# Feed-forward sums ahead of the block transposes, and routing ahead of the preceding group's, in a decoder layer in fp32

## The chip, the cores and the metric

The kernel runs on one core of a Trainium2 chip. The metric is the device time of one execution in microseconds (us). Before the change three runs gave 887.11, 887.35 and 888.24, a median of 887.35. Everything is fp32. The engines are called PE (matrix multiply; PEld is its weight load), DVE (vector), ACT (activations), POOL (GpSimd) and SP, which here only issues DMAs.

## What is computed

A decoder layer over 4096 tokens of width 256: 16 sequences of 256. Three sub-layers follow one another, each added to its input and normalised. The reference, cut to what matters:

```python
x = layernorm(x + attn(x))            # tokens against fixed keys and values, relu squared
x = layernorm(x + xattn(x, ctx))      # 16 heads of 16, softmax over 256 context rows
x = layernorm(x + ffn(x))

# xattn: attn = gamma * q @ k.T * scale + delta * (ap * max(D, 0) + an * min(D, 0))
#        D = clip(frac[k] - frac[q], -0.2, 0.2); out = softmax(attn) @ v @ Wo.T + bo

def ffn(x):                           # width 1024, 8 experts that differ by a rank 4 term
    logits = x @ gate_W.T + gate_b
    top1 = argmax(softmax(logits))
    base = x @ wi_W.T + wi_b
    for i in range(8):
        inter = relu(base + (x @ lora_A[i].T) @ lora_B[i].T)
        out += (top1 == i) * (inter @ wo_W.T + wo_b)
```

## The kernel before, in words

The program writes its order out by hand: within an engine the instructions run in the order in which the source issues them, and across engines they wait by semaphores for what they read and for buffers to come free.

The first sub-layer takes about the first 260 us. After it comes the main loop, which this change concerns. An iteration n handles one group: four of the sixteen heads of one sequence, 64 groups in all (n = 0 to 63, and two more iterations to drain). Several stages of different groups are interleaved. Group n is `now`, n + 1 is `nxt`, n - 1 is `last`, n - 2 is `older`:

- `negative` (POOL, L642, some on ACT) writes the negative part of the bias into `neg`, `positive` (ACT, L654) the positive part into four PSUM banks, one a head. `neg` has three buffers.
- `logits` (PE, L664) adds q.k to those banks. `maxima` (DVE, L682) adds `neg` and takes the row's extreme, bank by bank. `subtract` (POOL, L733) takes the maximum off heads 2 and 3.
- For heads 2 and 3, PE transposes the rows (`turned`, L743) and ACT takes the exponential into `pT` (`exps`, L750). For heads 0 and 1 of the groups 14 to 61 (`direct`) ACT takes it first (`exp_rows`, L696), then `blocks` (L707) transposes in blocks of 32 on DVE into `z` (one buffer, or the idle `kT` for every other group) and SP writes it to DRAM (`away_z`, L712). In the next iteration `fetch` (L724), four DMAs, brings it back in its final order into the same `pT`. SP's queue is in order: a fetch waits there for the landing of its write.
- `attend` (PE, L764), two iterations on as a rule, multiplies with the values into a PSUM bank `V`, heads 0 and 1 first, and `keep` (DVE, L777) copies it out. SP collects sums and values (L574 to L600), POOL divides (L607), PE projects (L614).

From n = 15 on the feed-forward of a block of 512 tokens (`ff`) is woven in, eight iterations, parts 0 to 7, per block; such a period is called a round here, rounds 0 to 5, with part = (n - 15) mod 8. Parts 0 and 1 transpose the block (L857, copied by ACT, L860) and multiply by gate and lora_A (`gates`, L872; copied by ACT, L882). Part 2 routes: `route` transposes the gates' result on PE (L887) and finds the first largest of eight on DVE in seven steps, lg (L893), top (L898), hot (L901, L902), first (L904), hot (L905) and `um` (four instructions, L909), the lora part masked by it. `biased` (POOL, L865) adds a bias to x. `inner` (L945) is the first large product, in two halves, `turn_um` (PE, L919, ACT's copy L925) transposes um, `lora` (L958) adds its product, and L967 (ACT) and L971 (DVE) apply the relu. Parts 4 to 7 `finish` 128 tokens each: eight matmuls (L978, sixteen PE instructions) and on DVE an add of the result to x (L991) and its mean and variance (bn_stats L191, bn_aggr L192). In parts 5 and 7 the result lies in the bank V that attend uses, and attend is put off by an iteration. In part 7 `prep` computes mean and scale of the next block on DVE (L208 to L246, the last is `nm`) and ACT scales its rows by them (L251).

`tile_b` hands out three PSUM banks in turn, so a transpose or product waits until the use three before it has been read. The blocks transpose of groups in parts 0 and 1 is put off (`later`) to the next iteration, after the maxima there. So in part 2 DVE runs the maxima, the preceding group's transpose into z, the routing, then the present group's transpose into kT. In parts 4 to 7 it runs, near the end of the iteration, the transpose and then the add and statistics of finish.

## Time and profile before

| | |
|---|---|
| median of three runs | 887.35 us |
| profiled execution | 887.49 us, of it the span of the profile 885.7 |
| granted PE clock, mean | 0.999 of full speed |
| PE waits in the whole span, longest in sum | attend L764 for the add L991: 6.0 us in 6 |
| maxima L682 on DVE | 512, 420 ns each |
| blocks transpose L707 on DVE | 24 into z, 1244 ns each; 24 into kT, 1238 ns each |
| add of finish L991 | 32, 381 to 422 ns; bn_stats L191 417 ns, bn_aggr L192 182 ns |
| routing: lg, top, hot, hot, first, hot, um | 162, 186, 503, 594, 186, 398 ns and four of 284 ns, 8 times |
| subtract L733 on POOL | 65, 1909 ns each |

In a timeline each row is start, duration, engine, line, operation, what is written and from what, with the idle time before it and who ended it in brackets. Times are counted from the start of the span. "issue" in such brackets means that the profile names nobody. SPq is SP's queue of DMA issues; when a DMA lands is told by the last of the sixteen updates of its semaphore in the trace. The ends of matmuls are modelled, so the start of what follows is the safer mark.

### The profile page before, as it was taken

The page shows a single profiled execution, that of the slowest core. Times are in us where ns is not written, and L with a number is a line of the kernel's source. Part 1 is how long each engine was busy: PE and PEld are TensorE (multiplying, and loading weights), DVE is VectorE, ACT ScalarE, POOL GpSimd, SP SyncE. Part 2 cuts the span into 40 slices and gives each one's busy share as a digit, 9 for nine tenths or more (in the row PEclk, how much of TensorE's full clock was granted, in tenths as well). Part 3 has the DMA queues.
Part 4 walks back from the last instruction along what each step waited for, and adds up shares of the span by engine and source line. Part 5 has one row for each costly group of instructions (what it writes and reads, how often), then busy time and mean ns, then how long its engine had stood idle before and what let it go on. Part 6 is the DMA issues. An engine that isn't in the chain of part 4 may idle for free.

```text
span 885.7 us, 20853 instructions
## 1 busy us (share of the span) xinstructions
PE 862.4 (97%) x7708; PEld 513.1 (58%) x7708; DVE 693.3 (78%) x1975; ACT 577.0 (65%) x1012; POOL 466.6 (53%) x455
## 2 busy tenths in 40 slices
PE   8999999999999999999999999999999999999997
PEld 4334444444456776567547656754765675576655
DVE  6878899889779898769778877877887787777444
ACT  5766777777788788647747765774875577475111
POOL 1100223322479898656828765883976678374010
PEclk9999999999999999999999999999999999999999
DMA  5501101010001333454454536445453644642001
GB/s 139 159 1 43 54 24 44 31 49 1 8 8 48 99 98 110 139 162 149 158 155 150 158 129 184 151 155 168 138 164 133 193 151 135 181 149 102 28 7 41
DMA packets 70373, 92.94 MB, mean 105 GB/s; under 512 B 13824, under 2 KB 55296, under 8 KB 70272
## 3 DMA queue, kind: packets, MB, share of 16 engines
q1 hardware_dynamic: 69696, 91.35, 33.2%
q8 instruction: 61, 1.00, 0.5%
q14 instruction: 40, 0.33, 0.1%
q10 hardware_dynamic: 576, 0.26, 0.1%
HBM read 50.43 MB, written 39.58 MB: 102 GB/s over the span
## 4 chain that ended last, share of the span: by engine, by line
PE 44%; DVE 11%; issue 2%; POOL 1%; ACT 1%; DMA 0%; ACTq 0%; POOLq 0%; DVEq 0%
PE ps_l L945 9%; PE ps_b L978 6%; PE ps_l L664 5%; PE ps_v L764 5%; PE ps_b L743 4%; DVE neg L682 3%; PE ps_b L614 3%; PE ps_v L978 3%; PE ps_b L477 2%; PE ps_l L958 2%; DVE z L707 1%; PE ps_b L503 1%; PE ps_b L532 1%; POOL neg L733 1%; DVE dpos L547 1%
## 5 line engine op out<-in xcount | busy, mean ns | idle before, releaser
L682 DVE CUSTOM_DVE_ANT_0 neg<-ps_l,neg 128x256 f32<-128x256 f32 x512 | 181.5, 420 | 41.4 <-PE ps_l L664 38.3
L642 POOL TENSOR_SCALAR neg<-dneg,aneg,delta 128x512 f32<-128x512 f32 x252 | 198.9, 804 | 20.9 <-PE ps_b L743 10.0
L654 ACT ACTIVATE ps_l<-dpos,apos_d 128x512 f32<-128x512 f32 x256 | 172.2, 688 | 49.9 <-DVE mx L682 30.9
L354 DVE TENSOR_TENSOR pr<-pr 128x1024 f32<-128x1024 f32 x128 | 153.8, 1243 | 30.2 <-ACT pr L353 29.8
L733 POOL TENSOR_TENSOR neg<-neg,mx 128x1024 f32<-128x1024 f32 x65 | 124.0, 1909 | 85.4 <-DVE mx L682 84.3
L353 ACT ACTIVATE pr<-ps_a 128x1024 f32<-128x1024 f32 x128 | 125.0, 1026 | 53.0 <-PE ps_a L345 52.7
L345 PE MATMUL ps_a<-xnT,kT 64*64 64x512 f32 x1024 | 124.6, 593 | 1.0 <-ACT xnT L330 0.4
L364 PE MATMUL ps_v<-pr,vv 64*64 64x512 f32 x1024 | 122.7, 589 | 0.0
L945 PE MATMUL ps_l<-xt,wi 128*128 128x512 f32 x248 | 111.7, 596 | 0.2
L750 ACT ACTIVATE pT<-ps_b 128x512 f32<-128x512 f32 x160 | 87.4, 590 | 32.4 <-PE ps_b L743 30.9
L743 PE MATMUL ps_b<-ident,neg 128*128 128x128 f32 x640 | 87.1, 277 | 3.4 <-ACT pT L750 2.3
L743 PEld LDWEIGHTS ps_b<-ident,neg 128*128 128x128 f32 x640 | 71.5, 141 | 24.0 <-issue 6.2
L364 PEld LDWEIGHTS ps_v<-pr,vv 64*64 64x64 f32 x1024 | 45.0, 133 | 64.5 <-issue 54.6
L379 POOL TENSOR_TENSOR xt<-xt,half 128x512 f32<-128x512 f32 x15 | 19.1, 1274 | 119.8 <-ACT half L378 119.8
L419 POOL TENSOR_TENSOR hid<-hid,bo 128x256 f32<-128x256 f32 x32 | 43.6, 1366 | 71.8 <-ACT hid L251 71.8
L696 ACT ACTIVATE neg<-neg,mx 128x256 f32<-128x256 f32 x192 | 81.3, 498 | 0.0
L764 PE MATMUL ps_v<-pT,vaug 128*32 128x256 f32 x1024 | 74.3, 385 | 7.2 <-DVE x L991 6.0
L664 PE MATMUL ps_l<-kM,qT 32*64 32x256 f32 x2048 | 79.8, 388 | 0.0
L345 PEld LDWEIGHTS ps_a<-xnT,kT 64*64 64x64 f32 x1024 | 41.9, 133 | 65.3 <-issue 52.5
L945 PEld LDWEIGHTS ps_l<-xt,wi 128*128 128x128 f32 x248 | 45.6, 191 | 49.4 <-issue 44.6
L978 PE MATMUL ps_b<-wof,hT 128*128 128x256 f32 x304 | 68.4, 380 | 0.0
L524 POOL TENSOR_SCALAR kM<-keys,of_head 128x512 f32<-128x512 f32 x22 | 38.7, 1760 | 48.4 <-DVE keys L513 48.4
(137 smaller groups left out, 1183.3 us busy)
## 6 DMA issues: line engine op xcount, KB each, us to landing
pT<-away_z SPq DMA_DIRECT2D x192, 128.0 KB
away_z<-z SPq DMA_DIRECT2D x24, 512.0 KB
away_z<-kT SPq DMA_DIRECT2D x24, 512.0 KB
away_v<-raw SPq DMA_DIRECT2D x16, 512.0 KB
cT<-in_ctxT SPq DMA_DIRECT2D x16, 256.0 KB
v<-away_v SPq DMA_DIRECT2D x32, 128.0 KB
invs<-rows SPq DMA_DIRECT2D x16, 256.0 KB
x<-in_x SPq DMA_DIRECT2D x7, 512.0 KB
```

The lines of the kernel that those rows point to most:

```text
L345: nc.tensor.matmul(sc[64 * k : 64 * k + 64, h, :], lhsT=kT[64 * h : 64 * h + 64, q, hf * P + 64 * k : hf * P + 64 * k + 64], rhs=self.xnT[ ...
L353: nc.scalar.activation(pr, sc, AF.Relu)
L354: nc.vector.tensor_tensor(pr, pr, pr, ALU.mult)
L364: nc.tensor.matmul(self.acc[k][64 * h : 64 * h + 64, :], lhsT=vv[64 * k : 64 * k + 64, hf, 64 * q : 64 * q + 64], rhs=pr[64 * k : 64 * k + ...
L642: nc.gpsimd.tensor_scalar(self.neg[:, g], self.batch.dneg, aneg[:, h : h + 1], delta, ALU.mult, ALU.mult,)
L654: nc.scalar.activation(banks[g], self.batch.dpos.rearrange("p j k -> p (j k)"), AF.Copy, scale=apos_d[:, h : h + 1],)
L664: nc.tensor.matmul(banks[g][64 * h : 64 * h + 64, j * S : (j + 1) * S], lhsT=self.batch.qT[rows, self.o, j * P + 64 * h : j * P + 64 * h + ...
L682: nc.vector.tensor_tensor_reduce(out=self.t[:, g, j, :], in0=banks[g][:, j * S : (j + 1) * S], in1=self.neg[:, g, j, :], scale=-1.0 if min ...
L733: eng.tensor_tensor(rows, rows, top.to_broadcast([P, 4, S]), ALU.subtract)
L743: nc.tensor.transpose(ps[:, k * S + j * P : k * S + (j + 1) * P], self.t[:, g, j, k * P : (k + 1) * P], ident,)
L945: nc.tensor.matmul(self.banks[g], lhsT=wi[:, c, f * P : (f + 1) * P], rhs=self.xT[:, c, :], start=(c == 0), stop=False,)
L978: nc.tensor.matmul(ps[:, 0:C], lhsT=self.hT[f][:, j * P : (j + 1) * P], rhs=wof[:, f, :], start=(f == 0), stop=(f == FC - 1),)
```

## The change

Two pieces move; nothing is added or removed.

```diff
             if now:
                 now.maxima()
                 now.later = n >= FIRST and part in (0, 1)
+            if ff and part == 2:
+                ff.route()
             if last and last.direct and last.later:
                 last.blocks()
...
                     last.turned(g)
                     last.exps(g)
-                if part == 2:
-                    ff.route()
                 if now.direct:
...
+            if ff and part >= 4:
+                ff.finish(part - 4, tile_v() if apart else None)
             if now and now.direct and not halved and not now.later:
                 now.blocks()
-            if ff and part >= 4:
-                ff.finish(part - 4, tile_v() if apart else None)
```

In part 2 of the six rounds the routing stands on DVE ahead of the preceding group's transpose, instead of between the two transposes; on PE its two transposes (L887) stand ahead of the eight of `turned` (L743), and with them its bank is taken from the three in turn ahead of theirs. In parts 4 to 7 the add and its statistics stand on DVE ahead of the present group's block transpose, in 23 iterations (in the last one, n = 62, there is no such transpose). The order on ACT, POOL and SP is as before.

## The prediction

> Times are microseconds (us) from the span's start. A round is the eight iterations of one feed-forward block, parts 0 to 7; the round shown, round 3, is n = 39 to 46, with its part 2 at 590 and its part 7 at 650.

> **What bounds the kernel now.** First the busy times of the page and the shares of the chain that ended last.

> ```profile
> PE 862.4 (97%) x7708; PEld 513.1 (58%) x7708; DVE 693.3 (78%) x1975; ACT 577.0 (65%) x1012; POOL 466.6 (53%) x455
> ...
> PE 44%; DVE 11%; issue 2%; POOL 1%; ACT 1%; DMA 0%; ACTq 0%; POOLq 0%; DVEq 0%
> ```

> PE is all but always busy, so what the change can win is what PE waits for. Next, therefore, PE's waits in the stretch 345 to 812, which holds every moved instruction (engine and line, whom it waited for, sum, times, longest).

> ```profile
> PE ps_v L764 <- DVE x L991: 6.0, 6, 1.6
> PE ps_b L919 <- DVE um L909: 2.6, 5, 0.5
> PE ps_b L503 <- DVE x L991: 0.7, 1, 0.7
> ```

> With 0.2 at L464 further down these 9.5 us are what the two moves aim at: the add L991 frees the bank that attend (L764) wants, and um (L909) feeds L919. The question of every step is what is late next.

> **Step 1, routing ahead of the preceding group's block transpose (6 places).** On DVE the transpose L707 (1.24 us) changes places with the seven steps of the routing; on PE two L887 go ahead of eight L743 (0.22 us later for those, whose reader ACT then has 4.49 us idle before umT). Taken simply, um comes 1.16 us earlier and the five waits of 0.52 us go. But look at the timeline of round 3 around the routing (start, duration, engine, line; the transpose z starts at 593.82):

> ```profile
> 594.05 1.90 POOL L733 TENSOR_TENSOR neg<-neg,mx 128x1024 f32<-128x1024 f32 x1 [0.49 <-DVE mx L682]
> ...
> 595.39 0.60 DVE L901 TENSOR_TENSOR hot<-lg,top 128x32 f32<-128x32 f32 x1
> ...
> 595.90 2.78 POOL L865 TENSOR_TENSOR x<-x,wofb 128x256 f32<-128x256 f32 x4
> 596.02 0.65 DVE L902 TENSOR_TENSOR hot<-hot,rev 128x32 f32<-128x32 f32 x1
> ```

> and at the same two lines in the last block, where POOL is idle:

> ```profile
> 848.55 0.19 DVE L901 TENSOR_TENSOR hot<-lg,top 128x32 f32<-128x32 f32 x1
> 848.78 0.19 DVE L902 TENSOR_TENSOR hot<-hot,rev 128x32 f32<-128x32 f32 x1
> ```

> The same 128x32 operation takes 0.19 us alone and 0.60 beside POOL, and it ends when POOL's operation does: L901 at 595.99, 0.05 after L733 (595.95); L902 at 596.67, just after the first of the four L865 (595.90 plus 0.73). So in six rounds of six. In the new order lg starts at 593.9 and L901 0.41 later, at 594.3. L733 waits for the last maximum and not for the transpose, so it starts at 594.05 as before, ahead of L901, which would then stand until 595.95 and end at 595.99: where it ends today. All that follows, um and L919 too, keeps its time. I take 0 for the gain. Bounds: nothing, or 5 x 0.52 = 2.6 if the 0.60 is a price that moves along with the operation.

> [...]

> The transpose z moves from 593.82 to 598.19, and kT from 598.19 to 599.43 (ends 600.67). DVE's next, L971, waits until 601.52 for L958, so 0.85 us of cover is left. On SP the two away_z writes go from 595.08 and 599.46 to about 599.5 and 600.7; what is queued behind them is sums at 604.22, and the fetches from 606.38, for attends at 614.97 and later. Nothing is late. POOL's L642 (598.66) must wait for z to release its neg buffer, 0.8 us; its next work is at 609.02. Cost: nothing.

> **Step 2, finish ahead of blocks in parts 4 to 7 (23 places).** Add, bn_stats and bn_aggr take 0.98 us of DVE; the transpose starts that much after the add, or later where the add itself must wait for L978. The bank comes free earlier by 1.2.

> (a) Attend in part 0, five of the six waits. Round 3:

> ```profile
> 651.34 2.08 ACT L251 ACTIVATE x<-hid,nm,rs 128x256 f32<-128x256 f32 x4 [1.17 <-DVE nm L246]
> ...
> 652.83 2.65 PE L764 MATMUL ps_v<-pT,vaug 128*32 128x256 f32 x32 [0.78 <-DVE x L991]
> ...
> 653.32 1.06 ACT L750 ACTIVATE pT<-ps_b 128x512 f32<-128x512 f32 x2
> ...
> 654.43 0.57 PEld L764 LDWEIGHTS ps_v<-pT,vaug 128*32 128x32 f32 x10 [0.34 <-ACT pT L750]
> ```

> The bank would be free at 651.60 and PE could start at 651.98. But the last ten weight loads wait for ACT's exps (end 654.38), ACT is behind L251, and L251 behind nm (L246, end 651.30), which stands ahead of both moved pieces. The stretch ends at 655.41 either way, in each of the five (all are 2.65 long, where an unstalled one takes 1.93). Gain 0 of 4.4. In round 1 the 0.67 at L503 goes the same way, since DVE's own chain sets nm there. The 0.16 at L464 in round 0 stays a gain.

> (b) Part 6, rounds 2 to 4: the transpose used to run while L978 ended (L978 ends 642.82, transpose 642.34). Now the add waits for it: 642.85, plus 0.98, plus 1.16 to the next start: maxima at 644.99 instead of 644.91. That path leads to nm and (a): 3 x 0.08 = +0.25.

> (c) The detour through DRAM. z is written away, fetched, and read by PE two iterations on. Round 0, part 7 (SP, then PE):

> ```profile
> 421.44 0.34 SPq L712 DMA_DIRECT2D away_z<-z  x1
> 425.05 1.82 SPq L724 DMA_DIRECT2D pT<-away_z  x4
> ```

> ```profile
> 430.01 1.55 PE L764 MATMUL ps_v<-pT,vaug 128*32 128x256 f32 x16 [0.24 <-issue]
> ```

> The last of the 16 semaphore updates of the last fetch is at 429.92, so this "issue" of 0.24 us is the transfer: PE starts 0.09 after it. In the other rounds PE starts 0.14, 0.57, 1.09 and 1.34 after. The transpose comes 0.98 later. Round 0: 429.92 + 0.98 - 0.17 (L464's gain) + 0.09 = 430.82, plus 1.00 for sixteen matmuls, 431.82 against 431.50 for the next instruction: +0.32. Round 1: 507.44 + 0.98 - 0.08 + 0.10 + 1.00 = 509.44 against 509.32: +0.12. In rounds 2 to 4 ACT's exps still end last: 0. Part 4's write comes 1.6 to 1.9 later and lands 0.4 to 1.4 ahead of its reader; part 6's likewise, under (a): 0.

> (d) Last round. No queries or keys are left, so PE is early: attend waits 1.63 at 788.23, the longest of the six. The bank is now free at 785.1 and PE starts at 786.54. But part 4's transpose moves from 778.20 to 780.12 (add at 779.14 when L978 ends), its fetch from 786.68 to 788.60, and the second sixteen start at 788.7 instead of 789.16: -0.4, not -1.6. Two iterations on the same again: L978 ends 0.4 earlier, at 795.15, part 6's transpose starts at 796.16 instead of 794.10, its fetch lands at 802.97 + 2.07 = 805.04; PE goes on at 805.14, plus 1.00, 806.14 against 805.13 today: +1.0 in place of the -0.4, and PE has no gap from there to the end that would absorb it.

> Sum: 0.32 + 0.12 + 0.25 + 1.0 = **+1.7 us**. The profiled execution took 887.49 (span 885.7), so 889.2; it lies 0.14 over the median of 887.35, to which 889.0 belongs.

> **Rivals.**
> 1. The 0.60 beside POOL moves along with L901: um is early, -2.6, and 1.7 - 2.6 = -0.9: 886.4. For it: only that no row has L901 start early in L733. Against: all six end times.
> 2. PE's named waits simply go: 6.0 + 2.6 + 0.9 = 9.5, 877.9 at the utmost. It decides only if ACT's exps for part 6's group end before 653.0, when PE would need them; against it they end at 654.38. A milder form, where the last round keeps its 1.6 because transfers land sooner and step 1 wins too (-4.2 + 0.7): 883.8.
> 3. The fetch becomes the bound in every round: decided by whether it lands over 0.1, 0.1, 0.6, 1.1 and 1.3 us later at PE's read. Writes took 2.6 to 3.7 us, by what v's reads do beside them; one more us at each place gives 1.3 + 1.1 + 0.6 + 0.2 = 3.2 for 0.4, and up to 1 more at the end: about +5, 892.4.

> **Numbers.** Forecast 0.52 (+0.3 to +3), rival 1 0.16, rival 2 0.08, rival 3 0.24. A measurement tells about 0.2% from no change, 1.8 us, and the forecast sits at that edge: 0.28 of it slower, 0.24 within. Slower 0.28 + 0.24 = 0.52; same 0.24 + 0.13 of rival 1 = 0.37; faster 0.08 + 0.03 = 0.11. The range 885.9 to 892.5 takes in both bounds of step 1 with the transfers' cost and rival 3, and leaves out rival 2 and the edges. The forecast's own: 887.7 to 890.4.

> **What would show it.** In the profile after, L901 still ends 0.05 after L733 and L919 still waits 0.5 for um (step 1); the wait of L764 for L991 is gone, but the weight loads wait for ACT pT longer, about 1.1 instead of 0.34 (a); PE's waits name DMA pT<-away_z or "issue" at L764 in rounds 0, 1 and twice in 5 (c, d); maxima of part 7 0.1 later against their L664 (b). I am wrong if L919's wait is gone, if the five long L764 stretches end earlier against the L664 before them, or if L724's landings do not follow the transposes.

## The result, and the profile after

Four executions of the changed kernel took 895.61, 900.30, 901.05 and 902.49 us, a median of 900.67; on the same chip the kernel before took 887.31. The ratio is 1.0139, with a 95% interval of 1.0098 to 1.0181: slower by 1.4%, some 13 us, where the forecast said +1.7. The profiled execution is the fastest of the four (895.61, span 893.8), 8.1 over the profiled one of before; so its trace explains 8 of the 13, and what makes the other executions longer has to be found too.

The page and PE's waits between 345 and 812 answer to those shown of before:

```profile
PE 862.5 (96%) x7708; PEld 513.7 (57%) x7708; DVE 698.4 (78%) x1975; ACT 577.1 (65%) x1012; POOL 465.6 (52%) x455
...
PE 38%; DVE 10%; DMA 7%; issue 2%; ACT 1%; SPq 1%; POOL 1%; ACTq 0%; DVEq 0%
```

```profile
PE ps_v L764 <- DMA pT<-away_z: 11.0, 11, 2.2
PE ps_b L919 <- DVE um L909: 2.6, 5, 0.5
PE ps_v L764 <- ACT pT L750: 2.6, 6, 0.6
PE ps_v L764 <- issue: 1.9, 1, 1.9
PE ps_v L764 <- DVE x L991: 0.6, 1, 0.6
```

The chain that had no DMA in it (0%) now has 7%. Attend's 6.0 us for the bank (L991) have shrunk to 0.6, and 11.0 us for the fetch stand in their place, with 1.9 named "issue" that are a fetch too. PE's busy time is the same: nothing was added, PE only waits longer.

To see where, I compared the start of each group's logits (L664) in the two traces. From n = 14 on the new one falls behind by 8.6 us in steps, each behind a wait of attend in the iteration before: +1.2 at n = 22, +1.2 at 25, +0.35 at 33, +0.2 at 41, +0.9 at 46, +1.1 at 49, +0.7 at 57, +4.0 behind the last L664; and small gains, -0.4 at n = 20 (L464), -0.7 at 31 (L503, given back by +0.6 at 32) and -0.5 at 62.

**Step 1 came out as worked out.** The routing of round 3 (compare the rows in the prediction):

```profile
595.93 1.89 POOL L733 TENSOR_TENSOR neg<-neg,mx 128x1024 f32<-128x1024 f32 x1 [0.71 <-DVE lg L893]
...
596.13 1.73 DVE L901 TENSOR_TENSOR hot<-lg,top 128x32 f32<-128x32 f32 x1
...
599.70 0.43 PE L919 MATMUL ps_b<-ident,um 128*128 128x128 f32 x2 [0.52 <-DVE um L909]
```

L901 starts 1.1 us earlier against L733 (0.20 us behind its start, where it was 1.34) and takes 1.73 us instead of 0.60; it ends at 597.86, 0.04 after L733 (597.82). So in six rounds of six; and L919 waits 0.52 for um in five of them, as it did.

**Three things were not foreseen.** The first is a write that takes longer. In parts 4 and 5 of all the profiles of this study (228 writes of 512 KB), one that meets nothing takes 2.63 us in the median, from issue to landing. The write of n = 19 took 2.62 before and 4.68 after. The two traffic rows below (GB/s, forty equal slices) are of the 5 us from 395 before and from 396 after; the writes are issued at 395.08 and 396.17.

```profile
GB/s 0 0 0 0 0 0 0 360 393 459 328 459 393 426 360 426 426 164 0 0 0 0 0 131 0 0 0 0 0 0 49 57 197 270 221 156 57 0 16 16
```

```profile
GB/s 0 0 0 0 0 0 0 0 459 393 360 328 393 590 360 426 262 459 33 0 0 0 33 0 0 33 0 33 33 0 33 33 33 33 0 0 0 0 0 0
...
q8 instruction: 1, 0.02, 1.3%
```

Both writes move their bulk in 1.3 us. The one of before is then done (the 131 after it is an instruction packet, the last bumps are the fetch). After, 33 GB/s trickle on for 2 us: in a slice of 0.125 us that is one 4 KB packet at a time, as I read it one of the sixteen DMA engines still at work. The updates of the write's semaphore say the same: before, all sixteen come within 2.62 us of the issue; after, fifteen come by 2.62 and the last alone at 4.68. The packet of 16 KB in queue q8, at 397.70, is, as I read it, what that engine had to move in between; q8 has 61 of them in the whole run, and between two of them start 255 of PE's instructions in the mean (255.3 before, 255.5 after; matmuls, weight loads and waits as the trace records them). So I take them for PE's instruction fetches. They come every 14.1 us before and 14.3 after, in the mean. In the changed kernel seven writes meet one 0.6 to 1.9 us after their issue (n = 17, 19, 28, 41, 43, 52, 61) and take 4.4 to 4.9; before it was one (n = 17), which had time.

The same happens to a fetch: in the changed kernel part 7's fetches of rounds 0 and 3 (issued at 426.38 and 659.85) met a packet 2.7 and 2.8 us after their issue and took 5.5 and 5.4 us, the other three 4.35 to 4.45.

The second is SP's queue; it is told with the experiments on part 6. The third is the clock. Attend and what follows it at the end of round 5 (PE's rows of the changed kernel), then the granted clock (the column after the five engines' busy times) in three stretches of 3.4 us:

```profile
810.79 1.28 PE L764 MATMUL ps_v<-pT,vaug 128*32 128x256 f32 x16 [2.22 <-DMA pT<-away_z]
812.01 1.97 PE L743 MATMUL ps_b<-ident,neg 128*128 128x128 f32 x8
813.77 1.61 PE L857 MATMUL ps_b<-ident,x 128*128 128x128 f32 x8
815.21 1.04 PE L743 MATMUL ps_b<-ident,neg 128*128 128x128 f32 x8
```

```profile
808.00:811.50 3.50, 1.28 (x28) 0.59 (x20) 2.93 (x17) 1.62 (x5) 1.80 (x1) 1.00 0.55 150
811.50:814.90 3.40, 3.40 (x22) 2.90 (x15) 2.67 (x7) 1.23 (x3) 0.09 (x1) 0.50 0.15 53
814.90:818.30 3.40, 3.40 (x32) 2.54 (x34) 0.93 (x3) 2.87 (x6) 0.00 (x0) 1.00 0.44 122
```

PE waits 2.22 us; then for 3.41 us the granted clock is 0.50, and eight transposes (L743) take 1.97 us, where eight like them take 1.04 a moment later. One such window loses half of 3.41, 1.7 us. The trace of before has none until 883.69, 2.0 us before its end. The other three executions of the changed kernel had mean clocks of 0.995, 0.994 and 0.992 against 0.998 of the profiled one; a window more is 0.0019 (1.7 of 895), so by an estimate from these figures they had some two to three windows more, 3 to 5 of the 5 to 7 us that they took longer.

### The profile page after: what moved, and what is told of

The parts are those of the page before. It is cut to its first block, busy times and chain, and to the rows that moved or that the text cites. A ratio compares the mean times of both kernels' runs of the same rounds, so it can differ in the third digit from the quotient of the medians.

```text
span 893.8 us, 20841 instructions
## 1 busy us (share of the span) xinstructions
PE 862.5 (96%) x7708; PEld 513.7 (57%) x7708; DVE 698.4 (78%) x1975; ACT 577.1 (65%) x1012; POOL 465.6 (52%) x455
## 4 chain that ended last, share of the span: by engine, by line
PE 38%; DVE 10%; DMA 7%; issue 2%; ACT 1%; SPq 1%; POOL 1%; ACTq 0%; DVEq 0%
PE ps_l L945 9%; PE ps_b L978 7%; DMA pT<-away_z 4%; PE ps_v L764 4%; PE ps_l L664 3%; PE ps_b L614 3%; DVE neg L682 3%; PE ps_b L743 2%; PE ps_l L958 2%; PE ps_b L477 2%; DMA away_z<-z 2%; PE ps_v L978 2%; DMA away_z<-kT 2%; SPq L724 1%; PE ps_b L503 1%
## 5 line engine op out<-in xcount | busy, mean ns | idle before, releaser
L642 POOL TENSOR_SCALAR neg<-dneg,aneg,delta 128x512 f32<-128x512 f32 x252 | 198.0, 801 | 31.1 <-PE ps_b L743 11.3
L682 DVE CUSTOM_DVE_ANT_0 neg<-ps_l,neg 128x256 f32<-128x256 f32 x512 | 180.9, 419 | 33.7 <-PE ps_l L664 33.5
L733 POOL TENSOR_TENSOR neg<-neg,mx 128x1024 f32<-128x1024 f32 x65 | 124.0, 1908 | 80.9 <-DVE mx L682 72.1
L750 ACT ACTIVATE pT<-ps_b 128x512 f32<-128x512 f32 x160 | 87.6, 590 | 40.1 <-PE ps_b L743 37.1
L743 PE MATMUL ps_b<-ident,neg 128*128 128x128 f32 x640 | 87.6, 278 | 3.0 <-ACT pT L750 2.3
L764 PE MATMUL ps_v<-pT,vaug 128*32 128x256 f32 x1024 | 74.0, 385 | 16.1 <-DMA pT<-away_z 11.0
L743 PEld LDWEIGHTS ps_b<-ident,neg 128*128 128x128 f32 x640 | 72.6, 142 | 21.5 <-ACT pT L750 4.9
L664 PE MATMUL ps_l<-kM,qT 32*64 32x256 f32 x2048 | 79.9, 388 | 0.0
L978 PE MATMUL ps_b<-wof,hT 128*128 128x256 f32 x304 | 68.4, 380 | 0.0
L764 PEld LDWEIGHTS ps_v<-pT,vaug 128*32 128x32 f32 x1024 | 29.6, 109 | 61.2 <-issue 36.5
```

The source lines that it names most:

```text
L642: nc.gpsimd.tensor_scalar(self.neg[:, g], self.batch.dneg, aneg[:, h : h + 1], delta, ALU.mult, ALU.mult,)
L682: nc.vector.tensor_tensor_reduce(out=self.t[:, g, j, :], in0=banks[g][:, j * S : (j + 1) * S], in1=self.neg[:, g, j, :], scale=-1.0 if min ...
L733: eng.tensor_tensor(rows, rows, top.to_broadcast([P, 4, S]), ALU.subtract)
L743: nc.tensor.transpose(ps[:, k * S + j * P : k * S + (j + 1) * P], self.t[:, g, j, k * P : (k + 1) * P], ident,)
L764: nc.tensor.matmul(to, lhsT=batch.va[:, k, self.head(g), :], rhs=rhs, start=(k == 0), stop=(k == 1),)
L978: nc.tensor.matmul(ps[:, 0:C], lhsT=self.hT[f][:, j * P : (j + 1) * P], rhs=wof[:, f, :], start=(f == 0), stop=(f == FC - 1),)
```

## The experiments

Each was run beside the kernel before on the same chip, whose median was 887.6 to 888.2; the ratios are to that, and times from different chips compare to about 1 us. "Steps" are delays of L664 against the trace of before, counted from n = 14.

### Which of the two moves

`e1_route_only` makes the first two hunks of the diff, `e2_finish_only` the third; `e3_parts_5_7` and `e4_parts_4_6` make the third for some parts:

```diff
+            early_sum = part in (5, 7)        # e4: part in (4, 6)
+            if ff and part >= 4 and early_sum:
+                ff.finish(part - 4, tile_v() if apart else None)
             if now and now.direct and not halved and not now.later:
                 now.blocks()
-            if ff and part >= 4:
+            if ff and part >= 4 and not early_sum:
                 ff.finish(part - 4, tile_v() if apart else None)
```

> The routing alone is moved ahead of the preceding group's block transpose; finish stays behind blocks. Theory A (late transfers: what costs is that the sums ahead of the block transposes bring those, and their way through DRAM, to attend too late): step 1 costs nothing, since um ends where POOL's L733 and L865 let it, so 887.3, within 1 us. Rival B (the routing's move has a share in the loss: L901 now stands 1.73 us and the two writes of part 2 go out back to back): at least 3 us more, 890 or over. L919 should wait 0.5 for um in five rounds by A and by B.

Measured: 888.15 us, 1.0003 (0.9994 to 1.0013). The routing costs and wins nothing.

> The sums alone are moved ahead of the block transposes, in parts 4 to 7; the routing stays. Theory A (late transfers): all of the loss, 895 to 903, with waits of L764 for pT<-away_z of about 10 us in sum. Rival B (the routing has a share): under 894.

Measured: 899.01, 1.0126 (1.0111 to 1.0141). All of the loss is in step 2.

> The sums are ahead of the block transpose only in parts 5 and 7, where the result lies in the bank that attend wants; in parts 4 and 6 they stay behind, and the routing stays. Theory A: the transposes of parts 4 and 6 keep their time, so their transfers land as before the change; part 7's come 1.0 later and cost 0.3 to 1 in rounds 0 and 1; the wait of 1.6 in the last round goes: 886 to 889. Rival C (every sum ahead of a transpose costs alike, about 1/23 of the loss each): half the loss, 893 or over.

Measured: 887.79, 0.9994 (0.9985 to 1.0003). Where the prediction had +0.32 and +0.12 in rounds 0 and 1, no step of as much as 0.1 us is seen; the wait in the last round is won (-1.49 at n = 62), and 0.5 is lost at n = 57.

> The sums are ahead of the block transpose only in parts 4 and 6, where the add must wait for L978 and the transpose moves by 1.0 to 2.1 us; in parts 5 and 7 they stay behind, and the routing stays. Theory A: most of the loss is here, 890 to 897, with waits of L764 for pT<-away_z in parts 6 and 0 and in the last round; the six waits of L764 for the add L991 stay. Rival C (every sum ahead costs alike): as in the kernel with parts 5 and 7 alone, about 893 both.

Measured: 900.39, 1.0136 (1.0084 to 1.0188), executions from 893.5 to 905.5: more than theory A expected (890 to 897). The profiled one had three windows at half clock, after PE had stood still for 2.1, 2.2 and 2.0 us of the window before each. Parts 4 and 6 lose as much as the whole change; parts 5 and 7 nothing that shows. Part 4 alone was not run.

### Part 6, and one place alone

`e6_part_6` has `early_sum = part == 6`, `e5_one_place` has `early_sum = n == 60`.

> The kernel before with the sum ahead of the transposes in part 6 alone (six places). Theory A (the loss grows at part 7's read: part 6's write comes later, the fetch that waits for it holds the DMA queue of SP, so v's reads are issued later and run beside part 7's write): 4 to 5.4 us for part 7's writes, attend of part 7 waits 1 to 3.5 us once a round, half-clock windows follow the longest of these waits; plus 6 to 12 us. Rival B (parts 4 and 6 each cost their own 1 us a round): plus 3 to 6 us, and part 7's writes as long as before (2.6 to 3.7).

Measured: 895.86, 1.0091 (1.0078 to 1.0105), steps of 8.2 us in sum. Theory A in size and in place, but not in the clock: no half-clock window came ahead of the end. SP's queue around part 7 of round 2, before and with part 6 alone moved (a write's length can be read here, since the fetch behind it is issued 0.12 and 0.13 us after its landing in the first of the two):

```profile
566.99 0.34 SPq L712 DMA_DIRECT2D away_z<-kT  x1
569.85 2.60 SPq L724 DMA_DIRECT2D pT<-away_z  x4
572.56 1.14 SPq L585 DMA_DIRECT2D v<-away_v  x2
...
575.88 0.34 SPq L712 DMA_DIRECT2D away_z<-z  x1
579.30 1.74 SPq L724 DMA_DIRECT2D pT<-away_z  x4
```

```profile
570.82 0.34 SPq L712 DMA_DIRECT2D away_z<-kT  x1
574.52 1.74 SPq L724 DMA_DIRECT2D pT<-away_z  x4
576.37 1.14 SPq L585 DMA_DIRECT2D v<-away_v  x2
...
578.28 0.34 SPq L712 DMA_DIRECT2D away_z<-z  x1
583.29 1.74 SPq L724 DMA_DIRECT2D pT<-away_z  x4
```

Part 6's write goes out 3.8 us later, with its group's transpose (2.3 of that is PE's own delay by then). It takes 3.57 us instead of 2.74 (an instruction fetch starts 0.34 after it; in rounds 0 and 1, without one, 2.98 and 3.10) and holds the fetch behind it; the fetch holds v's two reads (L585), so these start 1.9 us ahead of part 7's write, where they were 3.3 ahead. That write needs 4.89 us instead of 3.29, and PE waits 2.85 us for its group. Over all profiles, part 7's writes took 3.8 to 5.4 us where v's reads were issued less than 3 us ahead of them (14 writes); before, with 3.3 to 4.3 us between, they took 2.6 to 3.7.

The reads are not all of it. The fetch behind that write, issued at 583.29, took 6.02 us where the one of before took 4.27, because an instruction fetch met it 2.77 us after its issue: the last of its 64 semaphore updates came alone, 1.6 us behind the others. So too in rounds 0 (6.01) and 3 (5.45); in rounds 1 and 4 part 7's fetch met none and took 4.31 and 4.43. PE's waits for part 7's group in the five rounds are 2.19, 1.12, 2.85, 2.34 and 0.49, 9.0 in sum. By an estimate from these rows, writes of 2.62 us alone would have left 1.2 of that, and fetches of 4.36 alone 4.5.

> The kernel before with the sum ahead of the transposes at one place alone, n = 60 (part 5 of the last round), where attend waited 1.63 us for the bank. Theory A (a detour that is not delayed gives the bank's wait back): part 4's transposes stay where they were, so the fetch is not later; minus 1.3 to minus 1.6 us, ratio 0.9982 to 0.9986, no half-clock window. Rival B (any finish moved ahead makes some fetch late): ratio 1.000 or above.

Measured: 886.58, 0.9986 (0.9977 to 0.9995), a step of -1.50 at n = 62. Where the transposes of the groups around it are left alone, the bank's wait is really won: this is faster than both kernels, by 0.14%.

### v's reads out of the way

```diff
+            early_v = n % 8 == 6 and n >= 22           # e9, e10, e12: ahead of the fetch
+            if early_v:
+                batches[n // 4 - 1].regroup()
             if last and last.direct:
                 last.room()
                 if not last.later:
                     last.fetch()
-            if n % 4 == 2 and n >= 6:
+            if n % 4 == 2 and n >= 6 and not early_v:
                 batches[n // 4 - 1].regroup()
```

> The kernel with the sum moved in part 6 alone (which lost 8.2 us), and in part 7 of each round v's two reads (L585) issued ahead of the fetch of part 6's group and not behind it. Theory A (the late write of part 6 holds the fetch, the fetch holds v's reads in SP's queue, and these run beside part 7's write): v's reads are issued 2 to 4 us sooner, part 7's writes take 2.6 to 3.0 us instead of 4.1 to 4.9, PE's wait at attend of part 7's group falls from 1.1 to 2.9 us to 0.6 at most, median 888 to 890. Rival B (part 7's write is long because it comes closer behind part 6's own transfers): part 7's writes stay over 3.8 us, median 894 to 897.

Measured: 895.51, 1.0087 (1.0071 to 1.0103). Half of theory A came, its time did not. Part 7's writes fell to between 2.8 and 4.2 us and PE's wait for part 7's group is gone from the list, but v's reads now meet part 6's fetch, which takes 4.9 to 7.2 us instead of 4.2 to 4.4, and PE waits 0.5 to 1.5 us there in four rounds and 2.0 in the last; three half-clock windows follow. The meeting was moved, not removed.

> The changed kernel with the same move of v's reads. Theory A: the steps at part 7's group (1.2 + 0.35 + 0.2 + 1.1 + 0.7 us in the profiled execution) go, and with them the half-clock windows behind them; what an instruction fetch in a write costs (n = 19, 43, 61) stays: median 891 to 896, spread smaller than the changed kernel's 7 us. Rival B: 899 to 903, as the changed kernel.

Measured: 897.60, 1.0134 (1.0095 to 1.0173). Between the two theories, for the same reason: in the profiled execution part 7's writes are short (2.61 to 3.18 us), but part 6's fetches take 5.6 to 6.8 us, and PE waits 1.5 to 1.8 us a round for them. The spread grew to 10.6 us, where theory A had it shrink.

> The kernel before with the sum ahead at n = 60 alone (886.6) and v's reads issued ahead of part 6's fetch. Theory A: part 7's writes take 2.6 instead of 2.6 to 3.7 us, but PE waits there for the bank and for exps, not for the fetch, except by 0.1 to 0.25 us in rounds 0 and 1; 886.0 to 887.0, ratio 0.998 to 0.9995. Rival B (v's reads now lengthen part 6's write and delay its attend): 888 to 891.

Measured: 891.87, 1.0045 (1.0030 to 1.0060). Near rival B, but with the fetch in the place of the write: with part 6's transpose at its old place v's reads lengthen part 6's fetch to between 6.8 and 8.6 us, and this, with 6.8 us of half clock behind it in the profiled execution, costs 5 us over the one-place version.

The other way puts them one iteration later, behind the fetch of part 7's group (`e13`, `e14`, `e16`):

```diff
-            if n % 4 == 2 and n >= 6:
+            held = n % 8 == 6 and 22 <= n < 62
+            if n % 4 == 2 and n >= 6 and not held:
                 batches[n // 4 - 1].regroup()
+            if n % 8 == 7 and 23 <= n < 62:
+                batches[n // 4 - 1].regroup()
```

> The kernel with the sum moved in part 6 alone, and v's two reads of part 7 (L585) issued one iteration later, behind the fetch of part 7's group, in five of the six rounds. Theory A (the meeting of v's reads with the write or the fetch of a group is the whole loss of part 6): part 7's writes take 2.6 to 3.0 us, part 6's fetch 4.3 to 5 us, PE's waits at attend of part 7's group fall under 0.6 us, steps after n = 14 sum to 3 us at most, median 888 to 890.5. Rival B (the later place alone costs, 0.9 us a round and the end): 893 to 896. Rival C (v comes too late for the division and the projection): waits at L614 or of POOL's division, 890 and more, with new names among PE's waits.

Measured: 890.03, 1.0031 (1.0017 to 1.0044), steps of 1.9 us in sum instead of 8.2. Theory A; no new name among PE's waits from 345 to 830 (part 6 alone moved, without and with this):

```profile
PE ps_v L764 <- DMA pT<-away_z: 9.0, 6, 2.8
PE ps_v L764 <- DVE x L991: 6.9, 6, 1.8
...
PE ps_v L764 <- issue: 2.2, 1, 2.2
```

```profile
PE ps_v L764 <- DVE x L991: 6.9, 6, 1.8
...
PE ps_v L764 <- DMA pT<-away_z: 1.7, 2, 1.2
```

Of 11.2 us of waiting for the fetch 1.7 are left. Part 7's writes take 2.61 to 2.86 us; round 2, where v's reads now stand behind part 7's fetch:

```profile
575.64 0.34 SPq L712 DMA_DIRECT2D away_z<-z  x1
578.40 1.74 SPq L724 DMA_DIRECT2D pT<-away_z  x4
580.25 1.14 SPq L585 DMA_DIRECT2D v<-away_v  x2
```

Its fetches take 4.19 to 4.37, none of them lengthened by an instruction fetch; so the gain is in part where this run's instruction fetches happened to fall, and not only the move of the reads. What remains is mainly +1.4 in the last round, term (d) of the prediction.

> The changed kernel with v's reads behind part 7's fetch. Theory A: the steps at part 7's group go, those of n = 19, 43 and 61 (instruction fetches in a write) stay as far as they fall there again; no half-clock window but at the end: median 889.5 to 893, spread under 4 us. Rival B: 895 to 901.

Measured: 892.89, 1.0061 (1.0046 to 1.0077): 7.8 us less than the changed kernel. Part 7's writes take 2.61 to 2.96 us and its fetches 4.27 to 4.62, where the changed kernel had 3.40 to 4.05 and 4.35 to 5.49. The steps at part 7's group are gone, and no half-clock window comes before the end. The steps that are left are +1.2 at n = 22, +0.8 at 46 and +2.8 at the end, behind the writes of n = 19, 43 and 61, which took 4.70, 4.20 and 4.39 us beside an instruction fetch.

> The kernel before with the sum ahead at n = 60 alone and v's reads behind part 7's fetch. Part 7's writes 2.6 us instead of 2.6 to 3.7; PE waits there for exps, not for the fetch: as the one-place version, 886.0 to 887.0, ratio 0.998 to 0.9995. Rival (v too late): 888 and more.

Measured: 886.53, 0.9988 (0.9979 to 0.9997), as the one-place version.

### PE's instruction fetches

More transposes of nothing at the start shift all PE instructions against the fetches, between two of which start some 255 of them:

```diff
-WARM = 30
+WARM = 54        # e7, e17, e18; e11: 46
```

> The changed kernel with 24 more transposes of nothing at the start (54 for 30), 48 PE instructions more, so that PE's instruction fetches (16 KB for every 256 instructions) come at other places of the rounds. They cost about 4 us at the start. Theory A (three of the steps, 1.2 + 0.9 + 4.0 us, come from instruction fetches that fall into a write of z and lengthen it from 2.6 to 4.4 to 4.9 us): the writes of n = 19, 43 and 61 take 2.6 to 3.0 us, the loss after n = 14 shrinks from 8.6 to between 2 and 5 us, median 894 to 897. Rival B (only the place of the transposes counts): the loss after n = 14 stays 8 us or more, median 903 to 906.

Measured: 896.29, 1.0100 (1.0086 to 1.0114). The median is as theory A has it, the profiled execution not: the writes of n = 19, 43 and 61 fell to 2.61, 2.67 and 3.16 and their steps went (the end by +1.3), but other places were met instead (part 7's fetch of round 2 took 6.18 us), with two half-clock windows, and the steps sum to 9.3, not the 2 to 5 of theory A.

> The kernel before with 16 more transposes of nothing at the start (46 for 30), 32 PE instructions more, so that PE's instruction fetches come 1.5 to 1.9 us sooner. They cost 1.4 us at the start by the run with 24 more (2.1 us). Theory A (an instruction fetch that falls into a write costs 2 us of it, and the end where the fetch has no slack): nine writes are hit instead of one (n = 19, 22, 23, 28, 37, 43, 52, 57, 61) and take 4.0 to 5.0 us; the write of part 7 of round 0 (n = 22, no slack) gives a step of 1.5 to 2 us and n = 61 one of about 1; median 890.5 to 893. Rival B (instruction fetches only coincide): 888.5 to 889.5, no step after n = 14.

Measured: 890.09, 1.0027 (1.0014 to 1.0039). Inconclusive, between the two theories: in the profiled execution the instruction fetches came 2.4 us and more after seven of the nine writes, not 1 to 1.5. One of these seven took 4.76 us (n = 23), the others 2.6 to 3.3; the write of n = 52, met after 0.73 us, took 3.92. All had time, and the steps sum to 0.25. My estimate of how far 32 instructions shift them was wrong.

> The changed kernel with v's reads behind part 7's fetch and 54 transposes of nothing at the start for 30. Theory A (the three steps are instruction fetches in a write): the writes of n = 19, 43 and 61 take 2.6 to 3.2 us, the steps at n = 22 and 46 are under 0.3 us, that at the end 1.0 to 1.5; apart from the price of the longer start (see the kernel before with it) it is 2 to 3.5 us faster than without: 1 to 3 us over the kernel before with the same start. Rival B (the later place alone): the steps stay, 4.5 to 5.5 us over the kernel before with the same start.

Measured: 893.46, 1.0062 (1.0045 to 1.0079). The three writes took 2.61, 2.73 and 3.08 us, the steps at n = 22 and 46 are gone, the end is +1.3. From n = 17 on this execution loses nothing against the trace of before (-0.3); its 5 us are the longer start (2.1) and one step of 3.5 at n = 17. The median is not as theory A has it: 0.6 us over the same kernel with the shorter start, and under, not over, the kernel before with the same start, which follows.

> The kernel before with 54 transposes of nothing at the start for 30: the price of the longer start. About 2 us by the start of logits at n = 14 in the changed kernel with it; more where an instruction fetch now meets a write that has no slack (part 7 of round 0, n = 61): 889.5 to 892.

Measured: 896.73, 1.0094 (1.0071 to 1.0117): far more than expected, and the most telling run of all. Nothing is moved in it, and it loses 8.6 us, where the changed kernel loses 13.4. In its profiled execution, 9.0 us over that of before, 2.3 are the start. +3.5 come at n = 17, where an instruction fetch meets the fetch of n = 14 (6.0 us instead of 4.3) and a half-clock window follows. +3.4 come at n = 41 by the chain of part 6: an instruction fetch (2.31 us after the issue) makes part 6's write of n = 37 4.62 us long, v's reads start late, part 7's write takes 4.52, its fetch meets the next instruction fetch and takes 5.98, PE waits 2.44 us, and the clock halves. (The step at n = 17 is in e7 and e17 as well, so it belongs to the start.) SP's queue, from part 6's write to part 7's fetch:

```profile
572.67 0.34 SPq L712 DMA_DIRECT2D away_z<-kT  x1
577.42 1.74 SPq L724 DMA_DIRECT2D pT<-away_z  x4
...
581.57 0.34 SPq L712 DMA_DIRECT2D away_z<-z  x1
586.22 1.74 SPq L724 DMA_DIRECT2D pT<-away_z  x4
```

With the same start, then, the changed kernel (896.29, 1.0100) is no slower than the unchanged (896.73, 1.0094) as far as four executions each, on two chips, can tell; with v's reads behind part 7's fetch (893.46, on the unchanged one's chip) the median is 3.3 us lower.

### The clock

`e8_after_filled` adds two matmuls of nothing where PE waits (n = 24, 32, 40, 48, 56 and 63):

```diff
+                for _ in range(fill):
+                    nc.tensor.matmul(
+                        batch.av[:, self.i * S : (self.i + 1) * S],
+                        lhsT=ident, rhs=wq[:, 0, :], start=True, stop=True,
+                    )
...
-                older.attend()
+                older.attend(2 if n in (24, 32, 40, 48, 56, 63) else 0)
```

> The changed kernel with two matmuls of nothing (128x256, about 0.6 us each) ahead of attend at the six places where PE waits longest for the fetch (part 1 of each round after the first, and n = 63); what they write is overwritten. They stand in the wait, so they cost at most 0.3 us where the wait is shorter than they are. Theory A (a wait of about 2 us in a window of 3.41 us halves the clock in the next window, 1.7 us each, and the number of such windows makes the spread of the executions): no half-clock window between 345 and 820, median 894 to 897, spread under 3 us. Rival B (the clock falls for another reason, or the waits alone make the spread): windows at half clock stay, median 899 to 903.

Measured: 893.07, 1.0059 (1.0046 to 1.0073), executions from 892.55 to 893.67 at clocks of 0.999 to 1.0. More work, and 7.6 us less time: theory A, a little better than it expected. No half-clock window is left before the end, and the spread fell from 6.9 to 1.1 us. Not all of the 7.6 is the clock, for the 24 instructions also shifted the instruction fetches (the write of n = 61 took 3.19 us).

## Why the prediction was wrong

- **Step 1, right.** 0 as forecast, with the mechanism read from the rows: L901 took 1.73 us and ended 0.04 after L733. The run of the routing alone is at 1.0003.
- **(a) and (b), right.** The weight loads of attend in part 0 wait 0.67 to 1.05 us for ACT's exps (forecast about 1.1), so the 4.4 us for the bank are not won; the run with parts 5 and 7 alone shows no gain there either. The 0.08 a round of (b) is there, as steps of 0.08 to 0.09 at n = 40, 48 and 56 (plainest in e14). L503's 0.7 went and came back (-0.74, +0.61). L464 gave 0.38 instead of 0.16.
- **(c), the step that failed: "Part 4's write comes 1.6 to 1.9 later and lands 0.4 to 1.4 ahead of its reader; part 6's likewise, under (a): 0."** Only the moved transpose's own delay was carried through; each write was taken to need what it had needed before. Part 6's moved sum cost 8.2 us alone, for what stands behind its write on SP: a fetch, and behind that v's reads, which ran into part 7's write (4.1 to 4.9 us instead of 2.6 to 3.7); in three of five rounds part 7's fetch, now later, met an instruction fetch as well (5.5 to 6.0 us instead of 4.2 to 4.9). The prediction had named v's reads in rival 3 ("2.6 to 3.7 us, by what v's reads do beside them") but did not ask when a late write would issue them. The +0.32 and +0.12 forecast for part 7's own delay did not come: they are not there with parts 5 and 7 moved alone, nor with v's reads out of the way.
- **(c) again: the instruction fetches.** Three of the steps (n = 22, 46 and the end) stand behind writes that met one, and the two largest of the others (n = 25 and 49) behind fetches that did. In the trace of before only one write does, and its row there (4.79 us, n = 17) could have been asked for its reason.
- **(d), mechanism right.** -0.51 for a forecast -0.4 at n = 62, and +1.3 to +1.4 for +1.0 at the end where part 6's write took 3.1 to 3.2 us and the clock stayed full (e13, e17); 4.0 in the changed kernel, where the write took 4.4 and the clock halved.
- **The clock was not in the sum at all.** In the profiled execution a wait of 2.22 us was followed by 3.41 us at half clock, 1.7 us more.
- **Rival 3 was the case that came**, with its price too small: +5 for an extra microsecond at each place, where the writes got 2 us longer and the clock followed.

What stays open: only one execution of each kernel has a trace, so the shares of the three causes can be estimated for that one alone; no run moved v's reads while the instruction fetches stayed where they were, so the two are parted by estimate and not by experiment; part 4's share was not run by itself; and why an instruction fetch falls where it does was not settled: two shifts of the start moved it by other amounts than I had worked out.

## What to carry to other kernels

When a step is moved that ends in a DMA, follow the queue behind that DMA to its third and fourth entry and ask what each now runs beside; a write's length from another neighbourhood did not hold (part 7's 2.6 to 3.7 us became 4.1 to 4.9 with part 6's sum moved). Slack of less than 2 us at the end of such a chain was none here, where a write beside an instruction fetch took 4.4 to 4.9 us instead of 2.6: look for the writes that already take 2 us longer than their like, and for what they met. And a PE wait of about 2 us was dearer here than it looked, by the 1.7 us of the half-clock window behind it; with such waits filled the median was 7.6 us lower, though not all of it by the clock.
